# Two graph layers on one core: where the degree search, the edge counts, the sort and three groups of loads stand

## The chip, the cores and the metric

The kernel runs as one program on one core of a Trainium2 chip. The metric is the device time of one execution in microseconds (us); several runs give a median. The profile is of one further execution, taken by the hardware profiler. Its engines are called PE (matmul), PEld (PE's weight loads), DVE (vector), ACT (scalar), POOL (GpSimd) and SP (it only issues transfers); each of them executes its own stream of instructions in order.

## The reference

The input is a graph of 3125 nodes with 256 features and 100,000 directed edges, sorted by their target; the gates have an edge list of their own with 65,536 edges, which isn't sorted. Two layers follow, each of a graph network, a linear attention over all nodes and a group of experts, added to the features:

```python
xn = _layernorm(x, axis=-1)
x = x + _L0_gnn_ref(xn, edge_index, ...) + _L0_mix_ref(xn[None], ...)[0]
x = x + _L0_ffn_ref(_layernorm(x, axis=-1)[None], ..., L0_ffn_edge_index)[0]
xn = _layernorm(x, axis=-1)
x = x + _L1_gnn_ref(xn, edge_index, ...) + _L1_mix_ref(xn[None], ...)[0]
x = x + _L1_ffn_ref(_layernorm(x, axis=-1)[None], ...)[0]
```

A graph network is two convolutions with degrees normalized on both sides (the degree counts a node's incoming edges and itself):

```python
dinv = jnp.where(deg > 0, jax.lax.rsqrt(deg), 0.0)
norm = dinv[src] * dinv[dst]
hw = h @ W
msg = norm[:, None] * hw[src]
return jax.ops.segment_sum(msg, dst, num_segments=n) + b
```

Layer 0's attention is linear: keys and values are summed over all nodes into one context, which every query is multiplied with. Its experts (four, the best two of each node) are chosen by an attention over the gates' edge list. Layer 1's attention takes keys and queries to second order (`einsum('bhni,bhnj,bhne->bhije', kn, kn, vN)`); its eight experts are all computed and weighted by a softmax.

## The kernel before

The nodes are cut into 25 tiles of 128 (NT; the last has 53), and these into seven chunks of four tiles (CHUNKS; the last chunk has one). A convolution is a product with a dense adjacency matrix of edge counts, so it takes 25 steps k of one tile of sources for each chunk of targets. Every engine executes in order; the order is made by a list scheduler from the program, in which generators (`turns(work, n)` runs n steps of a piece of side work) weave side work into the main loops. A pool hands out SBUF from the left or (`**right`) from the right end; a tile that takes the space of an earlier one waits for that one's last readers.

The stages, in order of time in the profiled execution:

- 0 to 20 us: edge keys are made, and where each window of targets begins is searched for (`locate0`; its `find` is a search that counts smaller keys with ACT's Sign, gathers a row for each threshold by an indirect transfer on POOL, and counts in it again; the rows stand in a ring of tiles, `bufs`).
- 20 to 118: the kv phase of layer 0's attention, with LN on ACT (`layernorm(..., True)`), `to_columns`, keys, values and the context; `locate0` goes on beside it, four turns a chunk. Behind it stands `degrees0`: a second `find` with 25 thresholds, from whose counts come the degrees and `dinv`, with three turns of `counts` (the adjacency blocks, stage by stage: masks on DVE, products on PE, casts on ACT, a store to `cols`) for each of its turns.
- 122 to 254: the queries of layer 0's attention, tile by tile, with turns of `counts` and of `merging` (weights multiplied together). `feeder` loads rows of xn in fives and `split`s them, scaled by `dinv`, into a high and a low part (`hs`).
- 260 to 563: conv_1 (`conv_columns`, line 883, then `first_rows`). Ahead of each step k stand a split, the previous chunk's `first_rows`, counts for the next chunk, and the sort of the gates' edges (`sort1`: 512 keys on each of 128 partitions, min and max operations on DVE at lines 609, 610, 619 and 620, and from its tenth round on transposes `s_tp` on PE), `SORT[c]/4` turns a step. When the sort is through, `locate1` stores the keys (`ks1`), searches the windows and gathers them (`b_rows`, `b_got`), and `halves` transposes them (`b_gp`, line 360).
- 604 to about 820: conv_2 (`conv_rows`, line 904), with the counts of the gates' edges as side work. `blocks` and `wide_blocks` load an adjacency block (`adj`, line 856) and cast it (`adj_r`, line 859, ACT).
- 820 to about 1440: gates and four experts.
- 1440 to 1543: `project`: LN, the projections of layer 1's queries, keys and values, norms, and the stores of q, vk and hs to DRAM.
- 1549 to about 1815: mid_1, the first convolution with `key_sums` (products of key pairs, `kk` and `qa`, lines 2004 and 2013) as side work.
- 1815 to 2128: mid_2, the second convolution with layer 1's queries as side work: for each half of a chunk `q0`, four `left` and four `right` blocks are loaded (lines 2050 to 2061) and `gq`, `tt`, `yp` computed.
- 2152 to the end: `experts1`: 24 weight blocks of 0.26 MB on POOL's queue, then the first `prepare` (a load of x, LN, transposes, gates), then the eight experts for each chunk.

`project`, `layer1` and `experts1` are called one after the other; the pools of layer 1 (`l1`, `mid`, `mid_a`, `mid_1`, `mid_2`, `ffn`, `ffn_w`) are on the left, where project's pools are.

Of the kernel before, what the change touches and what calls it, by code (L numbers as in the profile page):

```python
# [17 lines left out]
P = 128  # L18
N = 3125
C = 256  # L20
NT = 25
# [34 lines left out]
PACE = 18  # L56
SORT = (2, 4, 5, 6, 6, 6, 8)
COLS = 782
# [37 lines left out]
def tile_gps_layers(ctx: ExitStack, tc: tile.TileContext, a: dict, out: bass.AP):  # L96
# [365 lines left out]

    def locate0(p, p3, ps, lo, hi, state):


        si = p.tile([P, COLS], I32, name="b_si")
        di = p.tile([P, COLS], I32, name="b_di")
        nxt = p.tile([P, 1], I32, name="b_nxt")
        full = E0 // COLS
        rest = E0 - full * COLS  # L470
        DVE.memset(si, 0)
        DVE.memset(di, N)
        DVE.memset(nxt, N)
        for t, name, queue in ((di, "dst", nc.sync), (si, "src", nc.scalar)):
            for r0, r1 in ((0, 112), (112, full)):
                queue.dma_start(t[r0:r1], a[name][r0 * COLS:r1 * COLS].rearrange("(p c) -> p c", c=COLS))
            queue.dma_start(t[full:full + 1, :rest], a[name][full * COLS:E0].rearrange("(p c) -> p c", p=1))
        with nc.allow_non_contiguous_dma(reason="the first of each row"):
            nc.scalar.dma_start(
                nxt[:full], bass.AP(tensor=a["dst"].tensor, offset=a["dst"].offset + COLS, ap=[[COLS, full], [1, 1]])  # L480
            )
        tabs = tables(p, ps, FAMILIES)
        next(tabs)
        yield

        DVE.tensor_scalar(di, di, N, None, op0=OP.min)
        DVE.tensor_scalar(si, si, N - 1, None, op0=OP.min)
        key = p.tile([P, COLS], F32, name="b_key")
        DVE.scalar_tensor_tensor(key, di, float(NPAD), si, op0=OP.mult, op1=OP.add)
        nc.sync.dma_start(ks[0:P * COLS, :].rearrange("(p c) o -> p (c o)", p=P), key)  # L490
        end = p.tile([P, 32], F32, name="b_end")
        DVE.memset(end, float(N * NPAD))
        nc.sync.dma_start(ks[P * COLS:, :].rearrange("(p c) o -> p (c o)", p=P), end)
        first = firsts(p, ps, key, SEG)
        base, thr, kcol, behind = next(tabs)
        nb = thr.shape[1]
        c = yield from find(p, p3, "w", 10, first, SEG, thr, nb, ks)
        got = gather(p, p3, c, kcol, ks, nb)
        yield
        thr_i = p.tile([P, NT], I32, name="b_thr_i")  # L500
        POOL.iota(thr_i, pattern=[[P, NT]], base=0, channel_multiplier=1)
        thr_n = p.tile([P, NT], F32, name="b_thr_n")
        DVE.tensor_scalar(thr_n, thr_i, float(N), float(NPAD), op0=OP.min, op1=OP.mult)
        yield from halves(p3, ps, got, base, lo, hi, "halves")
        state[:] = first, thr_n, di, nxt, key, got, behind

    def degrees0(p, p3, ps, want, state):

        first, thr_n, di, nxt, key, got, behind = state

# [4 lines left out]
        DVE.tensor_scalar(sh[:, 1], steps, float(P - 1), None, op0=OP.is_equal)  # L517
        c = yield from find(p, p3, "n", 10, first, SEG, thr_n, NT, ks)
        DVE.tensor_copy(begin[:, :NT], c)
# [10 lines left out]
        ranges = summed(FAMILIES)  # L530
        found = p.tile([P, 3 + 2 * len(ranges)], F32, name="b_found")
        wide = p.tile([P, COLS], BF16, name="b_wide")
# [4 lines left out]
        DVE.tensor_tensor(found[:, 1:2], nxt, di[:, COLS - 1:], op=OP.is_lt)  # L537
        over(p, got, behind, found[:, 2:3])
        for i, ends in enumerate(ranges):
# [304 lines left out]
    def wide_blocks(p):  # L844
# [5 lines left out]
        def make(i):  # L850
# [9 lines left out]
            made[i] = r  # L860

        make(0)
        for i, (ts, k0) in enumerate(steps_):
            make(i + 1)
            r = made.pop(i)
            for j in range(5):
                yield k0 + j, r[:, j]

# [605 lines left out]
    def counted(t):  # L1474
        while len(made) <= t and next(counts, 0) is None:
            pass

    with pool("where", **right) as wp, pool("where_w", **right) as wp3, pool("kv") as kp, \
            pool("kv_w", bufs=2) as mw, pool("ps_acc", space=PSUM) as psa:
        found_ = []  # L1480
        work = locate0(wp, wp3, psb, lo_b, hi_b, found_)
        turns(work, 1)
# [6 lines left out]
        for ts in CHUNKS:  # L1489
            xc = load_x(mw, ts)  # L1490
            turns(work, 4)
            xn = layernorm(mw, [xc[:, i, :] for i in range(len(ts))], True)
            ACT.activation(xc[:, :len(ts)], xn[:, :len(ts)], AF.Copy, bias=1.0)
# [21 lines left out]
        for g in range(2):  # L1515
            for h in range(4):
                s = slice(h * HD, (h + 1) * HD)
                DVE.tensor_copy(ctx_sb[s, g, s], ctx_ps[g][s, s])
                DVE.tensor_copy(ctx_sb[s, g, 128 + h:129 + h], ctx_ps[g][s, 128:129])
        for _ in degrees0(wp, wp3, psb, want, found_):  # L1520
            turns(counts, 3)

# [41 lines left out]
    hs = hp_.tile([P, NT, 2, C], F32R, name="hs")  # L1564
    feed = feeder(xp, hs, xn_dram, dinv)
    fed = (feed(k) for k in range(NT))

    with pool("merge") as gm, pool("mix_w", bufs=2) as mw, pool("ps_y", bufs=2, space=PSUM) as psy:
        merging = merged(gm, psm)
        turns(merging, 1)  # L1570
        for ts in CHUNKS:
# [6 lines left out]
            for g in range(2):  # L1578
# [8 lines left out]
                elu1(mw, qT[:, g, :w], qp[:, :w], [P, w])  # L1587
            for i, t in enumerate(ts):
                turns(counts, 1)
                op_ = psm.tile([P, 512], F32, name="op_", tag="a")  # L1590
# [111 lines left out]
    def general():  # L1702

        with pool("gat") as gp:
# [6 lines left out]
            with pool("moe", bufs=5) as mo, pool("moe_w") as ep, pool("moe_b", bufs=2) as mb, \  # L1711
                    pool("ps_e", bufs=2, space=PSUM) as ps:
                for step in moe0(mo, mb, ps, ps, "w", xT, load_e1(ep), *load_e2(ep)):
                    for _ in step:
                        pass
        for _ in project():
            pass
        layer1(False)

# [46 lines left out]
    def project():  # L1766
# [3 lines left out]
        with pool("proj") as pp, pool("proj_w", bufs=2) as cw, pool("ps_pr", bufs=2, space=PSUM) as ps:  # L1770
# [8 lines left out]
            for ts in CHUNKS:  # L1779
                n = len(ts)  # L1780
                c0, w = ts[0] * P, n * P
                xc = bring(cw, x_dram, ts)
                xn = layernorm(cw, [xc[:, i] for i in range(n)])
                xT = cw.tile([P, 2, 512], F32, name="xT")
# [7 lines left out]
                for i, t in enumerate(ts):  # L1792
                    r = rows_of(t)
                    cur = slice(i * P, (i + 1) * P)
                    qp = ps.tile([P, 512], F32, name="qp")
                    hp = ps.tile([P, 512], F32, name="hp")
# [50 lines left out]
    def experts1():  # L1847

        with pool("ffn") as fp, pool("ffn_w", bufs=2) as fw, pool("ps_f", bufs=3, space=PSUM) as ps, \
                pool("ps_fp", bufs=2, space=PSUM) as psp:  # L1850
# [4 lines left out]
            ws = [fp.tile([P, NE1, 2, C], F32, name="w_" + name) for name in names]  # L1855
            for e in range(NE1):
                for name, w in zip(names, ws):
                    nc.gpsimd.dma_start(w[:, e], a[name][e].rearrange("(k p) o -> p k o", p=P))

# [52 lines left out]
            got = []  # L1912
            for _ in prepare(chunks[0], got):
                pass
# [46 lines left out]

    def layer1(fast):
        with pool("l1") as lp:
            wpr = load_w(lp, "m1_wproj", 2)
# [80 lines left out]
            def queries(qw, pst, ps, ts, xc):  # L2045

                n, c0, w = len(ts), ts[0] * P, len(ts) * P
                oT = qw.tile([P, 2, 512], F32, name="oT", bufs=1)
                for g in range(2):
                    qc = q_dram[ts[0] // 4][:, 4 * g:4 * g + 4]  # L2050
                    q0 = qw.tile([P, 512], F32, name="q0", bufs=2)
                    nc.gpsimd.dma_start(q0[:, :w], qc[:HD].rearrange("j h w -> h j w"))

                    def four(name, bufs, at, by):
                        t = qw.tile([P, 4 * 512], F32, name=name, bufs=bufs)[:, :4 * w]
                        nc.gpsimd.dma_start(t, shifted(qc[at:], [HEADS * w, HD], [by * HEADS * w, 4], [1, 4 * w]))
                        return t
# [39 lines left out]

            def layer1_middle(fast):
                with pool("mid") as ch, pool("mid_a", bufs=2) as ca:
                    ahead = None  # L2100
                    if fast:
                        hs = ch.tile([P, NT, 2, C], F32R, name="hs")
                    else:
                        hs = ch.tile([P, NT, C], F32, name="hs_f")
                        hs4 = ch.tile([P, NT, C], F32, name="hs4")

                    def before(k):
                        if first and ahead:
                            ahead(k)
                        turns(work, 1)  # L2110

                    with pool("mid_1", bufs=2) as cw, pool("ps_c1", space=PSUM) as psc, \
                            pool("ps_cw1", bufs=2, space=PSUM) as ps, pool("ps_q1", space=PSUM) as psq:
                        work = key_sums(cw, psq, ps)
                        if fast:
                            ahead = feeder(ca, hs, hs_dram)
                        else:
                            nc.sync.dma_start(hs, hs_dram.rearrange("t p c -> p t c"))
                        gen = wide_blocks(ca) if fast else None
                        for ts in CHUNKS:  # L2120
# [21 lines left out]
                        for _ in work:  # L2142
                            pass
                    with pool("mid_2") as cw, pool("ps_c2", space=PSUM) as psc, \
                            pool("ps_cw2", bufs=2, space=PSUM) as ps, pool("ps_q2", space=PSUM) as pst:
# [19 lines left out]

            layer1_middle(fast)
            experts1()

    for _ in project():
        pass  # L2170
    layer1(True)
    slow = nc.values_load(slow_i[0:1, 0:1], min_val=0, max_val=1)
# [52 lines left out]
```

## Time and profile before

| | us |
|---|---|
| runs | 2729.72, 2735.25, 2735.89 |
| median | 2735.25 |
| the profiled execution's own time | 2732.49 |
| its span in the profile | 2730.7 |
| PE busy | 2492.9 (91%) |
| DVE busy | 1559.6 (57%) |
| ACT busy | 1356.6 (50%) |
| POOL busy | 169.1 (6%) |

The span is the time from the first to the last instruction in the profile; 1.8 us of the execution's time lie around it. The mean granted clock of PE was 0.944 of full speed. The chain that ended last, followed back from the end, is PE for 62% of the span, DVE for 7%, ACT for 5% and transfers for 3%.

Two further stretches are needed for the change, those of conv_1's chunks 0 and 1 (the columns are the stretch, its length, then the busy time and instructions of PE, PEld, DVE, ACT and POOL, the granted clock, the share of the DMA engines and GB/s):

```profile
260.00:280.00 20.00, 18.50 (x123) 14.63 (x123) 16.49 (x38) 9.47 (x9) 2.41 (x5) 0.91 0.55 193
280.00:300.00 20.00, 17.66 (x126) 12.97 (x125) 19.67 (x42) 6.50 (x9) 0.00 (x0) 0.95 0.21 85
300.00:320.00 20.00, 20.00 (x115) 14.19 (x114) 19.12 (x42) 14.10 (x18) 0.00 (x0) 0.97 0.64 205
320.00:340.00 20.00, 20.00 (x177) 15.49 (x176) 19.70 (x36) 13.27 (x24) 0.00 (x0) 1.00 0.37 145
```

The waits are read as a stretch of time in which an engine stood idle ahead of an instruction, with what ended the idling: "PE b_gp L360 <- DMA b_got" is PE, idle before the transposes of line 360, released when the transfer into b_got had landed; behind it are the sum in us, the number of such waits and the longest.

### The profile page before, as it was taken

The numbers are of one execution on the slowest core, as the hardware profiler recorded it, in microseconds if no ns is written. First come the engines' busy times: TensorE is split into PE (matmuls) and PEld (weight loads), VectorE is DVE, ScalarE is ACT, GpSimd is POOL, SyncE is SP. The second block draws the span as 40 slices with busy tenths as digits, with TensorE's granted clock in tenths as the row PEclk, the third lists the DMA queues.
The fourth block names the chain that finished last, engine by engine and source line by source line (L and its number), as shares of the span: only waits on it lengthen the run. The fifth ranks groups of instructions, "written<-read, shape, count | busy, mean of one in ns | idle before, by whom it ended". The sixth has DMA issues, their size and how long they took to land.

```text
span 2730.7 us, 33385 instructions
## 1 busy us (share of the span) xinstructions
PE 2492.9 (91%) x12351; PEld 1556.4 (57%) x12351; DVE 1559.6 (57%) x3626; ACT 1356.6 (50%) x2299; POOL 169.1 (6%) x234
## 2 busy tenths in 40 slices
PE   5788999959888799999979799999999699999999
PEld 3466777747674255555554376664555355555666
DVE  5678966547846756666549845547675422222221
ACT  5734566448857977777733444442332222222332
POOL 4411000010000000000001100011111200000000
PEclk8889999969999899999979899999999799999999
DMA  4434344346553111111015655369784300000000
GB/s 148 142 111 153 141 165 156 102 154 234 207 173 116 46 54 39 54 54 54 23 39 177 228 160 152 121 198 341 265 280 167 130 1 16 14 14 0 14 6 12
DMA packets 192591, 318.44 MB, mean 117 GB/s; under 512 B 12665, under 2 KB 165570, under 8 KB 186274
## 3 DMA queue, kind: packets, MB, share of 16 engines
q1 hardware_dynamic: 170930, 234.58, 26.2%
q0 software_dynamic: 17648, 77.12, 7.9%
q10 hardware_dynamic: 3840, 4.51, 0.5%
q8 instruction: 99, 1.62, 0.2%
q14 instruction: 74, 0.61, 0.1%
HBM read 229.40 MB, written 86.73 MB: 116 GB/s over the span
## 4 chain that ended last, share of the span: by engine, by line
PE 62%; DVE 7%; ACT 5%; DMA 3%; issue 1%; POOL 0%; SPq 0%; ACTq 0%; DVEq 0%; POOLq 0%
PE hp L1927 13%; PE acc L904 9%; PE yp L1139 7%; PE yp L1943 7%; PE acc L883 6%; PE hp L1125 5%; ACT pos L1277 2%; PE qa L2013 2%; PE tt L2084 2%; PE wb_p L1059 1%; PE by_s L1290 1%; PE b_bank L433 1%; DMA adj<-cols 1%; ACT adj_r L859 1%; DVE pos L1281 1%
## 5 line engine op out<-in xcount | busy, mean ns | idle before, releaser
L859 ACT CAST adj_r<-adj 128x2560 fp32r<-128x2560 bf16 (+1 forms) x140 | 293.1, 2104 | 245.8 <-PE acc L883 80.8
L904 PE MATMUL acc<-hs,adj_r 128*128 128x512 f32 (+1 forms) x1250 | 361.0, 420 | 13.3 <-DVE y L922 7.1
L883 PE MATMUL acc<-adj_r,hs 128*128 128x512 f32 (+1 forms) x1400 | 353.8, 398 | 4.2 <-ACT adj_r L859 4.2
L1277 ACT ACTIVATE pos<-drow,a_s 128x512 bf16<-128x512 f32 (+1 forms) x532 | 315.9, 665 | 78.2 <-PE by_s L1290 77.9
L1932 ACT ACTIVATE h<-hp,bn_b,bn_s 128x512 f32<-128x512 f32 (+2 forms) x224 | 160.9, 723 | 367.4 <-PE hp L1927 367.4
L904 PEld LDWEIGHTS acc<-hs,adj_r 128*128 128x128 f32 (+1 forms) x1250 | 224.7, 189 | 117.6 <-issue 54.7
L883 PEld LDWEIGHTS acc<-adj_r,hs 128*128 128x128 f32 x1400 | 248.5, 194 | 62.1 <-issue 8.3
L1946 DVE SCALAR_TENSOR_TENSOR xc<-yp,gate,xc 128x256 f32<-128x256 f32 (+1 forms) x200 | 95.1, 483 | 298.6 <-PE yp L1943 298.5
L1281 DVE TENSOR_TENSOR pos<-pos,adj 128x2048 bf16<-128x2048 bf16 (+1 forms) x133 | 146.9, 1107 | 122.6 <-ACT pos L1277 122.0
L1125 PE MATMUL hp<-g_xT,w 128*128 128x512 f32 (+1 forms) x448 | 195.9, 567 | 15.8 <-ACT hT L1128 14.1
L1139 PE MATMUL yp<-w,hT 128*128 128x256 f32 x800 | 208.4, 413 | 1.0 <-DVE xc_b L1140 1.0
L1943 PE MATMUL yp<-w_f_wo,h 128*128 128x256 f32 (+1 forms) x800 | 194.5, 386 | 0.3 <-ACT h L1932 0.2
L1927 PE MATMUL hp<-h,w_f_w 128*128 128x512 f32 (+2 forms) x448 | 185.8, 545 | 0.3
L1927 PE MATMUL hp<-xT,w_f_w 128*128 128x512 f32 (+2 forms) x448 | 184.0, 548 | 0.0
L403 DVE TENSOR_TENSOR b_ul<-lo_b,upto 128x2048 bf16<-128x2048 bf16 x117 | 143.7, 1228 | 67.8 <-PE b_bank L433 66.6
L1139 PEld LDWEIGHTS yp<-w,hT 128*128 128x128 f32 x800 | 158.8, 205 | 40.7 <-issue 15.9
L455 ACT CAST b_stage<-b_bank 128x500 bf16<-128x500 f32 (+7 forms) x323 | 151.3, 533 | 54.9 <-PE b_bank L433 53.8
L2004 DVE TENSOR_TENSOR kk<-vk 128x512 f32<-128x512 f32 (+1 forms) x200 | 125.6, 685 | 91.3 <-issue 51.3
L1943 PEld LDWEIGHTS yp<-w_f_wo,h 128*128 128x128 f32 (+1 forms) x800 | 142.5, 187 | 48.4 <-ACT h L1932 13.2
L433 PE MATMUL b_bank<-b_uh,b_ul 128*128 128x125 bf16 (+5 forms) x1856 | 139.6, 215 | 29.3 <-DVE b_uh L408 21.8
L433 PEld LDWEIGHTS <-b_ul 128*128 128x128 bf16 x1856 | 105.0, 102 | 81.7 <-issue 52.9
L1927 PEld LDWEIGHTS hp<-h,w_f_w 128*128 128x128 f32 x448 | 81.9, 190 | 94.0 <-issue 39.5
(566 smaller groups left out, 3446.9 us busy)
## 6 DMA issues: line engine op xcount, KB each, us to landing
adj<-cols SPq DMA_DIRECT2D x150, 640.0 KB, 4.6
cols<-b_stage SPq DMA_DIRECT2D x50, 800.0 KB, 4.5
left<-q_dram POOLq DMA_DIRECT2D x24, 1024.0 KB
right<-q_dram POOLq DMA_DIRECT2D x24, 1024.0 KB
xs_n<-hs_dram SPq DMA_DIRECT2D x15, 640.0 KB, 5.7
vk<-vk_dram SPq DMA_DIRECT2D x10, 840.0 KB, 4.8
vk_dram<-vk SPq DMA_DIRECT2D x6, 1344.0 KB, 5.0
x_in<-in_x SPq DMA_DIRECT2D x12, 512.0 KB, 6.1
```

Of the source, the lines that this page charges most:

```text
L433: PE.matmul(bank[:, n * NT:(n + w) * NT], u[:, i // 2, :, i % 2], v[:, i // 2, :NT * w, i % 2], start=k == 0, stop=k == room - 1,)
L455: ACT.copy(dst, src)
L859: ACT.copy(dst, src)
L883: PE.matmul(acc[f][:, :w], hs[:, k, q, s], at[:, :len(ts)], start=k == 0 and q == 0, stop=k == NT - 1 and q == 1,)
L904: PE.matmul(acc[i][:r, :], at[:, i, :r], hs[:, k].rearrange("p q c -> p (q c)"), start=k == 0, stop=k == NT - 1,)
L1125: PE.matmul(hp[:, :w], w1[:, e, k, f * P:(f + 1) * P], xT[:, k, c0:c0 + w], start=k == 0, stop=k == 1)
L1139: PE.matmul(yp[:, :C], hT[:, f, i * P:(i + 1) * P], w2[:, e, f, :], start=f == 0, stop=f == 3)
L1277: ACT.activation(pos[:, h, :n].rearrange("p t d -> p (t d)"), drow[:, h, :w], AF.Sign, bias=a_s[:, k, h:h + 1],)
L1281: DVE.tensor_mul(pos[:, :, :n], pos[:, :, :n], at[:, None].to_broadcast([P, 4, n, P]))
L1927: PE.matmul(hp[:, :w], ws[layer][:, e, k, f * P:(f + 1) * P], h[:, k, :w], start=k == 0, stop=k == 1,)
L1932: ACT.activation(hn[:, f, :w], hp[:, :w], AF.Relu, bias=bn[layer][1][:, at:at + 1], scale=bn[layer][0][:, at:at + 1],)
L1943: PE.matmul(yp[:r, :C], h[:, k, i * P:i * P + r], ws[2][:, e, k, :], start=k == 0, stop=k == 1)
```

## The change

Five things are moved; what is computed stays the same.

1. The sort of the gates' edges gets more turns in each of conv_1's chunks (SORT), so it stands earlier in the order.
2. `degrees0` is a generator that is now run one turn for each tile of the queries, and its tiles and those it takes over from `locate0` come from a pool of their own (`degrees`, `pd`); its ring of rows has 6 tiles and not 10. `over` (a check of the windows) moves into `locate0`. The counts that stood with the degrees are run in the kv phase instead, four turns a chunk from tile 12 on, and LN of the first three chunks there is done on DVE. The feeder is made when its first turn is asked for.
3. Layer 1's pools go to the right end. `project` is a generator that is run for six of its seven chunks; then layer 1's pools are opened, the feeder and the first adjacency block are made, and only then the seventh chunk is run. `project`'s LN goes to ACT, and the first tile's `qp` is taken ahead of LN.
4. The ten loads of the first chunk's queries in mid_2 go from POOL's queue to SP's.
5. The 24 weight loads of `experts1` go from POOL's queue to SP's, and stand behind the first step of the first `prepare` (the load of x and LN) in the program.

```diff
-SORT = (2, 4, 5, 6, 6, 6, 8)
+SORT = (4, 5, 7, 7, 8, 8, 8)
...
-    def locate0(p, p3, ps, lo, hi, state):
+    def locate0(p, p3, pd, ps, lo, hi, state):
...
+        found = pd.tile([P, 3 + 2 * len(summed(FAMILIES))], F32, name="b_found")
+        over(p, got, behind, found[:, 2:3])
+        state[:] = first, thr_n, di, nxt, key, found
...
-        c = yield from find(p, p3, "n", 10, first, SEG, thr_n, NT, ks)
+        c = yield from find(p, p3, "n", 6, first, SEG, thr_n, NT, ks)
...
+        def each():
+            for i, (ts, k0) in enumerate(steps_):
+                make(i + 1)
+                r = made.pop(i)
+                for j in range(5):
+                    yield k0 + j, r[:, j]
+
         make(0)
-        for i, (ts, k0) in enumerate(steps_):
-            make(i + 1)
-            r = made.pop(i)
-            for j in range(5):
-                yield k0 + j, r[:, j]
+        return each()
...
             turns(work, 4)
-            xn = layernorm(mw, [xc[:, i, :] for i in range(len(ts))], True)
+            if ts[0] >= 12:
+                turns(counts, 4)
+            xn = layernorm(mw, [xc[:, i, :] for i in range(len(ts))], ts[0] >= 12)
...
-        for _ in degrees0(wp, wp3, psb, want, found_):
-            turns(counts, 3)
+        for _ in work:
+            pass
...
-    feed = feeder(xp, hs, xn_dram, dinv)
-    fed = (feed(k) for k in range(NT))
+
+    def feeding():
+        feed = feeder(xp, hs, xn_dram, dinv)
+        for k in range(NT):
+            feed(k)
+            yield
+
+    fed = feeding()
...
+        degrees = degrees0(wd, wd, psb, want, found_)
...
             for i, t in enumerate(ts):
+                turns(degrees, 1)
                 turns(counts, 1)
...
-                xn = layernorm(cw, [xc[:, i] for i in range(n)])
+                qp = ps.tile([P, 512], F32, name="qp")
+                xn = layernorm(cw, [xc[:, i] for i in range(n)], True)
...
-            for e in range(NE1):
-                for name, w in zip(names, ws):
-                    nc.gpsimd.dma_start(w[:, e], a[name][e].rearrange("(k p) o -> p k o", p=P))
...
-            for _ in prepare(chunks[0], got):
+            first = prepare(chunks[0], got)
+            next(first)
+            for e in range(NE1):
+                for name, w in zip(names, ws):
+                    nc.sync.dma_start(w[:, e], a[name][e].rearrange("(k p) o -> p k o", p=P))
+            for _ in first:
                 pass
...
+                    queue = nc.gpsimd if ts[0] else nc.sync
...
-                        nc.gpsimd.dma_start(t, shifted(qc[at:], [HEADS * w, HD], [by * HEADS * w, 4], [1, 4 * w]))
+                        queue.dma_start(t, shifted(qc[at:], [HEADS * w, HD], [by * HEADS * w, 4], [1, 4 * w]))
...
+                    if fast:
+                        ahead = feeder(ca, hs, hs_dram)
+                        gen = wide_blocks(ca)
+                    for _ in rest:
+                        pass
...
-    for _ in project():
-        pass
-    layer1(True)
+    maps = project()
+    turns(maps, len(CHUNKS) - 1)
+    layer1(True, maps)
```

## The prediction

> **What bounds the kernel now.** I read the busy shares first, then the stretches where they drop, then the waits and the chain in those. PE works 91% of the span:
>
> ```profile
> span 2730.7 us, 33385 instructions
> PE 2492.9 (91%) x12351; PEld 1556.4 (57%) x12351; DVE 1559.6 (57%) x3626; ACT 1356.6 (50%) x2299; POOL 169.1 (6%) x234
> PE   5788999959888799999979799999999699999999
> PEclk8889999969999899999979899999999799999999
> ```
>
> Outside the first 120 us, PE's digits dip at slices 8, 20 to 22 and 31: the turn from conv_1 to conv_2 in layer 0 (from 560 us), from project to the first convolution of layer 1 (from 1540) and from mid_2 to the experts (from 2128). There is also a shallower stretch after the kv phase (120 to 160). The stretches themselves (columns: span; busy time of PE, PEld, DVE, ACT, POOL; granted clock; DMA share; GB/s):
>
> ```profile
> 120.00:140.00 20.00, 10.26 (x85) 6.45 (x84) 14.38 (x36) 8.88 (x24) 13.30 (x8) 0.68 0.65 221
> ...
> 560.00:580.00 20.00, 7.36 (x32) 6.18 (x31) 7.23 (x28) 6.59 (x23) 4.83 (x5) 0.67 0.41 140
> 580.00:600.00 20.00, 4.71 (x25) 3.02 (x26) 10.96 (x28) 5.42 (x15) 4.82 (x6) 0.50 0.40 122
> 600.00:620.00 20.00, 17.93 (x103) 13.72 (x101) 8.93 (x10) 14.89 (x19) 0.00 (x0) 0.79 0.54 182
> ...
> 1540.00:1550.00 10.00, 4.46 (x34) 2.64 (x38) 7.11 (x23) 3.04 (x7) 0.63 (x1) 0.68 0.59 222
> 1550.00:1560.00 10.00, 6.41 (x148) 3.43 (x144) 8.90 (x20) 2.88 (x9) 0.00 (x0) 0.98 0.79 263
> 1560.00:1570.00 10.00, 6.01 (x32) 3.10 (x25) 10.00 (x24) 7.99 (x14) 0.00 (x0) 0.54 1.00 339
> ...
> 2140.00:2150.00 10.00, 0.00 (x0) 0.00 (x0) 2.34 (x15) 0.00 (x0) 7.74 (x11) 0.50 1.04 348
> ```
>
> No engine is full where PE idles, so these are waits. What ended them, PE's waits at 520 to 606 and at 2120 to 2166, with two steps of the chain:
>
> ```profile
> PE b_gp L360 <- DMA b_got<-ks,b_ci: 20.8, 5, 17.6
> PE s_tp L648 <- DVE s_key L610: 5.5, 2, 4.0
> ...
> PE tr L187 <- DVE ln_xn L176: 23.6, 1, 23.6
> ...
> 1825.72 16.22 DMA q<-q_dram
> ...
> 2131.36 18.30 DMA xc<-x_dram
> ```
>
> After the sort's last stage (565.0 us) come the store of the keys, two rounds of gathers and the table products; only then does conv_2's first matmul (604.43) get its block. At the end of mid_2, LN waits for an 18.3 us load of x's rows.
>
> **The change, part by part.**
>
> *Sort sooner.* SORT[c]/4 turns per k step, 25 steps a chunk: 12, 25, 31, 37, 37, 37, 50 before, 229 in all; now 25, 31, 43, 43, 50, 50, 50, or 292. The sort has 229 yields and the search 16 more; the sum passes 229 thirteen turns before chunk 5 ends and 245 just after. In the built program the gathers stand 4 to 8 matmuls into chunk 6 (of 50). Before, chunk 5 ended about 528 and the sort 565, and its tail took 565 to 592.7, the b_gp wait's end: 27.7 us. Started at 528 it ends near 556, before chunk 6 (563). What still stands before conv_2 is the last hw2 (569.55), adj's load (4.6 us by the DMA issues) and a cast of 2.23: 576.4 instead of 604.4. PE's idle in 560 to 620 is 12.64 + 15.29 + 2.07 = 30.0; about 7 stay, so I take 24. Upper bound 35 (all idle, and the 5.5 of s_tp waits). Lower bound 8: in SP's order adj now stands behind two xc loads, a store of hs, xs_n and a store of cols1, and three landings of 5 us in a row would add 15.
> The price: a stage is two DVE operations, 0.417 to 0.421 us each (L609, L610), so 0.84. Chunk 0 gets 13 more turns: 10.9 us, where DVE was idle only 3.5 + 0.3 of 260 to 300. That is 7 us late, between 0 (PE has 1.5 and 2.3 idle there already) and 10.9. Chunks 2 to 5 gain 6 to 13 turns each, under 11 us, against DVE's 24 to 30 busy of 40: hidden. If not, PE stops at the transposes s_tp, which stand in its own order. Net 17.
>
> *Degrees amid queries, counts amid keys.* The degree search moves 25 gathers (POOL), 100 small ACT operations (0.51, 0.20, 0.63, 0.19: 38 us) and its three DVE steps from the end of the kv phase into the queries; 16 turns of counts move into the kv phase, and LN of the first three chunks from ACT to DVE. PE's idle in 120 to 160 is 9.74 + 4.67 = 14.4, the most there is. But DVE is busy 17 to 19 of each 20 us from 160 to 260, so degrees must stay cheap there, and the built program still issues all 25 gathers before the kv phase ends, with dinv ready ten feed steps later than before. I take 6, between 15 and -5: POOL and ACT stand at 0 and 9.5 of 20 after 140 and dinv is needed only from 250 on, but the 5.6 us that DVE idles in 120 to 140 are then lost to a search that lands on a full DVE. The ring of gather tiles falls from 10 to 6, cost nothing under the same idle POOL.
>
> *Layer 1's pools and project's last tile.* Six chunks of project, then the feeder's loads, splits and the first adj load and cast, then the one-tile chunk. In the built order PE goes from project's last transposes straight to acc. Idle in 1540 to 1570 is 5.54 + 3.59 + 3.99 = 13.1. Ten hs splits (0.42 us each, 4.2 in all) move into a project whose DVE has 9.8 of each 10 us busy: I take 12 less 2. LN moves there from DVE to ACT (25 x 0.43, L176 there, = 10.7 us off DVE; on ACT 25 x 0.56, L174 in the kv phase, = 14.0, hidden under its 4.3 of 10): PE idles only some 5%, so 2. Net 12, between 5 and 17.
>
> *First queries on SP.* Ten loads, 2 x (0.25 + 4 x 1.02) = 8.7 MB, leave POOL's queue for SP's, behind hs's store and xc, ahead of xs_n and the fifth adj. POOL was held until 1824.11; on SP they can go from about 1819. But 8.7 MB at the 348 GB/s shown above is 25 us either way, and SP stops at the fourth `right` until DVE frees a buffer, so xs_n and adj come some 10 us later. I take 2, between -5 and 6. The Trainium skill (DMA: Bandwidth & Descriptors, "Issuing engines are not separate DMA queues") says that SP, ACT and GpSimd feed the same 16 DMA engines, so that another issuer saves issue time alone; the stretch at a share of 1.04 agrees, and by that rule this part would be worth 0.
>
> *Experts' start.* 24 weight loads of 0.26 MB leave POOL for SP. Before they shared the DMA engines with three xc loads, all issued from 2130.18; LN's last input landed at 2149.8. Now eight of them stand ahead of the first xc on SP, the other xc's behind all 24. Eight are 2.1 MB or 6.0 us at 348 GB/s; they can begin at 2127.2 (the last acc), xc adds 0.5 MB or 1.5, so it lands near 2135 and at worst, behind a wait of SP for the last row's store (3.5 us there), near 2139: 15 or 11 us sooner. Allow 3 to 15 and take 10: the clock stays cold at such a gap (0.50 there). The Trainium skill (TensorE: Matmul & The Clock Gate, "What's actually happening") puts the drop to half rate at about 3.4 us of idling. By that rule too the 10 us that remain bring no gain of clock here, while the gap at 1560, closed whole, would.
> Clock: the 6 us of work at 0.54 in 1560 to 1570 at full speed save 2.8. I add 3.
>
> Sum: 17 + 6 + 12 + 2 + 10 + 3 = 50. The profiled execution was 2732.49 (1.8 around its span), 2.8 under the median 2735.25; 2732.5 - 50 = 2682.5, on the median's footing 2685.
>
> **The rivals.**
> 1. *The sort's tail only shrinks*: adj behind SP's row of loads (the lower bound 8) and DVE's lateness of 10.9 eat that part, and the experts' xc gains only 3: 50 - 20 - 7 = 23, so 2712. For it: SP's in-order queue. Against: the loads ahead are not blocked in 555 to 570.
> 2. *Everything arrives*: the upper bounds, 35 - 7 + 15 + 17 + 6 + 15 + 3 = 84, so 2651. For it: PE is the only full engine, and all of this is its idle time. Against: DVE's 97% in 280 to 340, and the 10 us that the experts' first load takes in any case.
> 3. *The degrees do not move in effect*, since their gathers still stand in the kv phase: that term 0, 2691.
> 4. *Slower*: the denser sort makes PE wait at its transposes. Fourteen s_tp groups (seven rounds of two) stand in PE's order; one wait was 4.0 us at worst, with 50 turns a chunk. If all fourteen pay that, 56, and chunk 0 pays 10.9 instead of 7, the sum is 50 - 56 - 4 = -10: 2745. It decides from 3.6 us per transpose on. For it: chunks 4 to 6 now all run at 50 turns. Against: only 2 of 14 waited in 520 to 606, when nothing was left behind them, and DVE has 10 to 15 us of 40 free in chunks 2 to 5.
>
> **Numbers.** My forecast 0.55 (2670 to 2702, with rival 3 inside it), rival 1 0.22, rival 2 0.10, rival 4 0.08, and 0.05 for the terms adding up to nothing. The range 2655 to 2715 takes in rival 1 and reaches almost to rival 2; it leaves out rival 4, the nothing case and the edges of the others. A measurement here tells apart about 0.3%, 8 us. Faster 0.88, same 0.04, slower 0.08.
>
> **What would show it.** conv_2's first acc 24 to 30 us after conv_1's last, not 41, with b_gp's wait under 3 us; s_tp waits under 10 us in all (above 40, rival 4); acc of mid_1 right after project's last transposes; PE's wait for ln_xn before the experts 10 to 15 us; and the kv phase's end followed by a stretch with less than 7 of 20 us idle on PE. I am wrong if the queries grow by more than 6 us or if mid_2's start waits longer for xs_n than it gains.

## The result, and the profile after

The changed kernel took 2700.65 us (median of four runs, 2691.64 to 2711.03); the kernel before, run beside it, 2732.48. The ratio is 0.9886, with a 95% interval from 0.9843 to 0.9929. The profiled execution took 2696.51 us, 36.0 less than that of before (2732.49). One thing ahead of the rest: the text on the kernel before says four `left` and four `right` loads for each half of a chunk; it is two and two, each of four shifted blocks (1.02 MB).

The page of the changed kernel, its busy times and slices:

```profile
span 2694.7 us, 33358 instructions
PE 2488.3 (92%) x12351; PEld 1548.0 (57%) x12351; DVE 1558.3 (58%) x3617; ACT 1362.4 (51%) x2312; POOL 143.6 (5%) x200
...
PE   5887999889988899999879999989999799999998
```

PE has nearly the work that it had (2488.3 us against 2492.9); its idle time fell from 237.8 us to 206.4. Counted from 0, slice 8 has gone from 5 to 8, and the 7s of slices 20 and 22 have shrunk to one; slice 26, in mid_2, has a new 8 among 9s. The stages' ends, from the two traces' PE records (us of the span):

| | before | changed | moved |
|---|---|---|---|
| kv phase, last ctx ends | 118.5 | 120.0 | +1.5 |
| queries, last ty ends | 254.6 | 235.2 | -19.4 |
| conv_1, first acc starts | 260.2 | 249.4 | -10.8 |
| conv_1, last acc ends | 561.0 | 552.7 | -8.3 |
| conv_2, first acc starts | 604.4 | 573.2 | -31.2 |
| conv_2, last acc ends | 838.2 | 804.4 | -33.8 |
| gates, last by_s ends | 1415.5 | 1380.6 | -34.9 |
| mid_1, second chunk ends | 1632.9 | 1597.1 | -35.8 |
| mid_1, last acc ends | 1815.2 | 1775.5 | -39.7 |
| mid_2, last acc ends | 2126.9 | 2101.1 | -25.8 |
| experts, first gate product | 2154.1 | 2118.9 | -35.2 |
| end of the last yp | 2724.2 | 2687.9 | -36.3 |

Read by differences: 10.8 us came from the front; conv_1 grew by 2.5; 25.5 came between conv_1's end and conv_2's, 22.9 of them at the turn; 1.1 came in the gates, next to nothing (0.9) from project and mid_1's start, 3.9 in the rest of mid_1; mid_2 lost 13.9; and the experts' start brought 9.4 to their first product, 10.5 to the end.

Stretches of the changed kernel that answer to those shown of before (same columns), and PE's waits in 500 to 575, in 1770 to 1852 and in 2095 to 2125:

```profile
120.00:130.00 10.00, 7.78 (x29) 3.87 (x29) 8.38 (x24) 2.81 (x6) 3.65 (x2) 0.66 0.71 255
130.00:140.00 10.00, 9.20 (x87) 7.20 (x84) 9.13 (x29) 3.02 (x7) 1.47 (x1) 1.00 0.01 2
...
540.00:560.00 20.00, 17.52 (x129) 16.44 (x129) 11.78 (x28) 10.51 (x28) 0.96 (x1) 0.93 0.76 250
560.00:580.00 20.00, 14.65 (x91) 10.99 (x90) 9.44 (x10) 13.45 (x21) 0.00 (x0) 0.81 0.73 240
...
1510.00:1520.00 10.00, 4.75 (x18) 2.33 (x16) 8.84 (x30) 3.88 (x11) 0.63 (x1) 0.82 0.52 185
1520.00:1530.00 10.00, 10.00 (x46) 8.17 (x46) 1.45 (x5) 3.65 (x5) 0.00 (x0) 0.84 0.58 209
...
1820.00:1830.00 10.00, 5.65 (x28) 0.88 (x27) 10.00 (x5) 0.78 (x3) 1.80 (x3) 0.83 0.98 306
```

```profile
PE b_gp L360 <- DMA b_got<-ks,b_ci: 3.7, 3, 2.4
...
PE gq L2080 <- DMA q<-q_dram: 6.2, 2, 5.3
PE tt L2101 <- DVE qq L2092: 3.5, 4, 1.4
...
PE tr L187 <- DVE ln_xn L176: 14.1, 1, 14.1
```

The wait for the gathers fell from 20.8 us to 3.7 and the wait before the experts from 23.6 to 14.1. PE is busy at 1520, where before it idled until 1566. But at 1820 it is half idle at a DMA share of 0.98. The chain of waits in mid_2's first chunk shows why:

```profile
1783.90 18.70 DMA q<-q_dram
1802.60 28.29 DMA adj<-cols
1830.89 0.02 issue
1830.91 2.33 ACT adj_r L859
```

An adj load that takes 4.2 us at the median took 28.3 here: it was issued on SP behind the ten loads of queries, and beside the next chunk's on POOL.

### The profile page after: what moved, and what is told of

The parts are those of the page before. It is cut to its first block, busy times and chain, and to the rows that moved or that the text cites. A ratio compares the mean times of both kernels' runs of the same rounds, so it can differ in the third digit from the quotient of the medians.

```text
span 2694.7 us, 33358 instructions
## 1 busy us (share of the span) xinstructions
PE 2488.3 (92%) x12351; PEld 1548.0 (57%) x12351; DVE 1558.3 (58%) x3617; ACT 1362.4 (51%) x2312; POOL 143.6 (5%) x200
## 4 chain that ended last, share of the span: by engine, by line
PE 62%; DVE 7%; ACT 5%; DMA 4%; issue 1%; SPq 0%; ACTq 0%; DVEq 0%
PE hp L1943 13%; PE acc L907 9%; PE yp L1142 7%; PE yp L1959 7%; PE acc L886 6%; PE hp L1128 5%; DMA adj<-cols 3%; PE qa L2029 2%; ACT pos L1280 2%; PE tt L2101 1%; PE wb_p L1062 1%; PE by_s L1293 1%; ACT adj_r L859 1%; PE b_bank L433 1%; DVE pos L1284 1%
## 5 line engine op out<-in xcount | busy, mean ns | idle before, releaser
L886 PEld LDWEIGHTS acc<-adj_r,hs 128*128 128x128 f32 x1400 | 245.4, 192 | 63.7 <-issue 13.1
L1128 PE MATMUL hp<-g_xT,w 128*128 128x512 f32 (+1 forms) x448 | 195.4, 566 | 15.1 <-ACT hT L1131 13.4
```

The lines of the kernel that those rows point to most:

```text
L886: PE.matmul(acc[f][:, :w], hs[:, k, q, s], at[:, :len(ts)], start=k == 0 and q == 0, stop=k == NT - 1 and q == 1,)
L1128: PE.matmul(hp[:, :w], w1[:, e, k, f * P:(f + 1) * P], xT[:, k, c0:c0 + w], start=k == 0, stop=k == 1)
```

## The experiments

Stage lengths are those of each run's profile. "Gates to mid_1" is the stretch from the gates' end to the end of mid_1's second chunk (before 217.5, changed 216.5), "first two" the length of mid_2's first two chunks (109.2 and 124.0). Where a time is set beside the changed kernel's, "the eight runs" are those four and four of e4, which has the same order of instructions (median 2707.9).

**e1.** The queries' loads back on POOL:

```diff
-                    queue = nc.gpsimd if ts[0] else nc.sync
+                    queue = nc.gpsimd
```

> The changed kernel with the ten loads of mid_2's first query chunk back on POOL's queue; all else as changed. In the changed kernel mid_2's chunk 0 took 71.8 us (1777.0 to 1848.8) against 41.6 before, and one adj load there took 28.3 us; over mid_2 11 us were lost. Theory A: on SP the ten loads (8.7 MB) stand ahead of xs_n and adj, so the convolution waits for them; back on POOL's queue chunk 0 takes 40 to 48 us, no adj load there over 12 us on the chain, and the time falls by 8 to 12 us. Theory B: the loss comes from mid_1's earlier end (all stores and loads of the turn falling together at the DMA engines' limit); then chunk 0 still takes over 60 us and the time changes by less than 4 us.

Measured: 2712.97 us (ratio to before 0.9918, interval 0.9889 to 0.9946). mid_2's first chunk 59.9 us, the first two 129.1, mid_2 342.7. Theory A failed: with the pools where the change puts them, POOL's queue is no better. Theory B came in part: the first chunk is just under its 60 us, but the time is 12.3 us above the changed kernel's (5.1 above the eight runs), where under 4 was said. SP's waits in 1770 to 1815, then POOL's, then those of the kernel before (SP's and POOL's in 1810 to 1850):

```profile
SPq L703 <- DMA hs_dram<-new: 21.2, 1, 21.2
...
POOL left L2073 <- DVE h4T L2149: 259.5, 1, 259.5
```

```profile
SPq L703 <- DMA hs_dram<-new: 4.5, 1, 4.5
...
POOL left L2056 <- DMA hs_dram<-new: 25.2, 1, 25.2
```

Before, POOL's second `left` waited for mid_1's last store of hs, because of the space that it took; so the store (0.13 MB) went without the queries, in 4.5 us, and xs_n followed; only q0 and the first `left` had gone out earlier. With the pools at the right end the same load waits for another reader (`h4T`), is free 3.6 us ahead of the store, and the store, which SP waits for before xs_n, takes 21.2 us beside 6.4 MB of queries (seven loads; the expectation of e5 counts 4.3 MB).

**e2.** The sort's old turns:

```diff
-SORT = (4, 5, 7, 7, 8, 8, 8)
+SORT = (2, 4, 5, 6, 6, 6, 8)
```

> The changed kernel with the old turns for the sort (2, 4, 5, 6, 6, 6, 8). Theory A: the sort's tail comes back behind conv_1: conv_2's first acc 40 to 44 us after conv_1's last (20.5 in the changed kernel), and conv_1 becomes 1 to 3 us shorter: the time rises by 20 to 25 us. Theory B: a good part of the 25 us comes from degrees and counts being out of the way sooner; then the gap is under 35 us and the time rises by less than 15 us.

Measured: 2727.38 us (0.9984, 0.9964 to 1.0003). From conv_1's last acc to conv_2's first 41.1 us (20.5 changed, 43.4 before), conv_2's end 19.4 us later, conv_1 299.7 us long against 303.3. PE's wait for b_got in 500 to 592 is back:

```profile
PE b_gp L360 <- DMA b_got<-ks,b_ci: 18.7, 4, 16.4
PE s_tp L648 <- DVE s_key L610: 5.8, 2, 4.4
```

Theory A: the tail is the sort's alone; the time rises by 26.7 us, by 19.5 against the eight runs. The denser sort's price in conv_1 is 3.6 us, and it falls into chunk 1 (54.6 us in the changed kernel, 48.0 here), not into chunk 0 (30.8 and 32.2).

**e3.** Degrees, counts, the kv phase's LN and the feeder as before (all hunks of part 2 undone).

> The changed kernel with degrees0, counts, the kv phase's LN and the feeder as before. In the changed kernel the last ty of the queries ends 19.4 us sooner, conv_1's first acc 10.8 us sooner and its last 8.3 us sooner. Theory A: this part is worth what conv_1's first acc shows: first acc near 260 us, the time 8 to 11 us longer. Theory B: conv_1's start is set by DVE's queue of counts, not by the queries; what comes sooner there is paid back by conv_1's end, and the time rises by less than 5 us.

Measured: 2723.29 us (0.9956, 0.9933 to 0.9979). conv_1's first acc at 257.9 (+8.5), its last at 566.0 (+13.3), conv_2's end 9.1 us later: theory A, for the stages. The profiled execution is 26.1 us longer than the changed kernel's, and the rest stands in stages of which this edit changes no line: 9.9 in mid_2 (335.5 us against 325.6), 4.1 in the gates, 2.9 in the experts.

**e4.** Project run whole:

```diff
-    turns(maps, len(CHUNKS) - 1)
+    turns(maps, len(CHUNKS))
```

> The changed kernel with all seven chunks of project run before layer 1's pools are opened (the pools stay at the right end, LN stays on ACT). In the changed kernel the stretch from the gates' end to the end of mid_1's chunk 1 takes 216.5 us against 217.4 before: the idle time of PE between project and mid_1 is gone, but project is 6.4 us longer. Theory A: the two belong together: with the feeder's splits and loads behind project again, project is 4 to 7 us shorter and the gap comes back, the time changes by less than 3 us. Theory B: the longer project is due to LN on ACT alone, and the weaving is worth the whole gap: the time rises by 7 to 12 us.

Measured: 2712.09 us (0.9911, 0.988 to 0.9941), gates to mid_1 216.1. The scheduler made the same streams from it (the same on DVE and SP; on PE and ACT only a weight tile's number differs), so neither theory was tried: writing the last chunk behind the feeder changes no order. The run is worth more as a repetition. Its mid_2 took 340.2 us, the changed kernel's 325.6, from the same order of instructions. The eight runs of the two have a median of 2707.9, so by the medians the change is worth rather 24 to 32 us than 36.

**e5.** The queries on POOL, with a dependency of the first half's five loads on that store:

```diff
+                    if not (ts[0] or g):
+                        after(load, kept)
...
+                                kept[:] = [nc.sync.dma_start(
+                                    hs_dram[ts[0]:ts[0] + n].rearrange("t p c -> p t c"), new[:, :n]
+                                )]
```

> The changed kernel with the first queries' ten loads on POOL's queue, the five of the first half made to wait for mid_1's last store of hs. With them on POOL's queue and no such wait, mid_2 took 342.7 us (from mid_1's last acc to mid_2's last), 325.6 in the changed kernel, 311.7 before; there the store of hs took 21.2 us behind 4.3 MB of query loads that had started 3.6 us ahead of it (4.5 before, where POOL itself had waited 25.2 us for that store), and xs_n waited for the store. Theory A: what counts is that the store and xs_n are not behind the queries' data; the store takes under 7 us, mid_2 takes 308 to 318 us and the time falls by 8 to 14 us against the changed kernel. Theory B: mid_2 is longer for a reason that this order does not touch (where its tiles now lie, the loads' rate); it takes 325 us or more again.

Measured: 2705.87 us (0.9905, 0.9869 to 0.994). The store's wait was 4.5 us again and the first chunk 51.7 us (73.3 changed), but the second took 72.4: first two 124.1, mid_2 333.4, in the range of theory B (325 or more). Theory A fails as it was put. Part of that lies in the edit: q0 waited for the store too; ACT then stood 8.5 us before an operation on q0 and with it the casts of adj.

**e6.** Layer 1's pools at the left end again, opened when project's are closed (`turns(maps, len(CHUNKS) + 1)` and `**right` taken from l1, mid, mid_a, mid_1 and mid_2), queries on POOL.

> The changed kernel with layer 1's pools (l1, mid, mid_a, mid_1, mid_2) at the left end again and opened behind all of project, and the first queries on POOL's queue; LN of project stays on ACT, the experts' pools at the right end. Theory A: the place of the pools is what did both: closed the gap between project and mid_1 and let the queries' loads start ahead of the store of hs. So the gap is back (first acc 149 to 153 us after the gates' end, 139.6 in the changed kernel), project itself is shorter by 4 to 7 us, the gates' end to mid_1's second chunk takes 215 to 219 us as in both kernels, and mid_2 takes 308 to 318 us: the time falls by 8 to 14 us against the changed kernel. Theory B: the pools' place closed the gap for nothing else: the stretch to mid_1's second chunk is 223 us or more, and mid_2's gain is eaten.

Measured: 2690.04 us (2686.02 to 2696.8; 0.9836, 0.9818 to 0.9854). The first acc is 154.9 us after the gates' end, gates to mid_1 221.2, the first two 115.6, mid_2 317.4. Both halves of theory A came, the gap and mid_2's gain, but three of its figures were missed: the first acc is later than 149 to 153, project is only 2.5 us shorter (last qp at 126.7 against 129.2, 4 to 7 said), and gates to mid_1 is over 219. So 4.7 us are lost to mid_1, but mid_2 gains more. The waits are those of before: POOL's in 1782 to 1830, PE's in 1500 to 1545, and PE's of the kernel before in 1536 to 1570:

```profile
POOL left L2073 <- DMA hs_dram<-new: 25.6, 1, 25.6
...
PE qa L2029 <- DVE kk L2020: 6.4, 6, 2.1
PE tr L187 <- DVE qf L1845: 5.2, 4, 4.2
...
PE qa L2013 <- DVE kk L2004: 7.6, 7, 2.1
PE tr L187 <- DVE qf L1831: 5.5, 5, 4.2
```

**e7.** The experts' weights on POOL's queue, ahead of `prepare`, as before.

> The changed kernel with the experts' 24 weight loads on POOL's queue and at their old place in the program. In the changed kernel the stretch from mid_2's last acc to the experts' first gate product is 17.8 us, 27.3 before. Theory A: the queue decides, since on SP the first load of x has only eight weights ahead of it, and on POOL all 24 share the DMA engines with it: 26 to 29 us, the time 8 to 11 us longer. Theory B: it is the experts' pools at the right end that let loads start sooner: 17 to 21 us, and the time within 3 us of the changed kernel's.

Measured: 2719.64 us (0.9938, 0.9914 to 0.9962). From mid_2's last acc to the first gate product 27.8 us (17.8 changed): theory A for this stretch. Of the 27.0 us by which the profiled execution is longer, the other 16.5 stand in mid_2 (342.1), which comes ahead of these loads. PE's wait in 2112 to 2150, and the step of the chain:

```profile
PE tr L187 <- DVE ln_xn L176: 24.1, 1, 24.1
...
2122.26 18.95 DMA xc<-x_dram
```

In the changed kernel the same load of x took 5.81 us of the chain.

**e8.** No counts in the kv phase:

```diff
-            if ts[0] >= 12:
-                turns(counts, 4)
```

> The changed kernel without the four turns of counts a chunk in the kv phase, so that these 16 turns fall to the queries and conv_1; degrees as changed. In the changed kernel the kv phase ends 1.5 us later, the queries 19.4 us sooner and conv_1's first acc 10.8 us sooner than before. Theory A: the queries are bound by DVE and the counts moved under the kv phase are what shortened them: the queries end 10 us or more later than in the changed kernel, conv_1's first acc 5 to 12 us later. Theory B: the degrees' waits, gone from the turn between the phases, are what shortened them: the queries end less than 5 us later and conv_1 starts less than 4 us later.

Measured: 2726.88 us (0.9985, 0.9959 to 1.001). The kv phase ends 8.3 us sooner (111.7), the queries at 235.9, hardly later, but conv_1's first acc comes at 268.9, 19.5 us later. So B for the queries and more than A for conv_1. Three stretches in between and PE's wait in 230 to 272:

```profile
240.00:250.00 10.00, 4.22 (x51) 3.84 (x49) 10.00 (x23) 0.00 (x0) 0.00 (x0) 0.50 0.16 51
250.00:260.00 10.00, 4.75 (x80) 4.41 (x79) 9.94 (x28) 3.32 (x7) 0.00 (x0) 0.50 0.33 135
260.00:270.00 10.00, 3.59 (x51) 3.29 (x52) 10.00 (x19) 5.12 (x5) 0.00 (x0) 0.50 0.50 164
```

```profile
PE b_bank L433 <- DVE b_uh L408: 19.5, 13, 3.2
```

DVE is full (10 of 10 us), most of it with the masks of the counts that conv_1 must have. What decides conv_1's start is this queue, not the queries. The rest of part 2 by itself would have made it later than before (268.9 against 260.2); the counts under the kv phase, for 8.3 us there, save 19.5.

**e9.** The kernel of e6 with project's LN on DVE (the `True` of the diff taken out).

> The kernel of e6 (layer 1's pools at the left end behind project, first queries on POOL's queue) with project's LN on DVE as before. In e6 project's last qp starts 126.7 us after the gates' end, in the kernel before 122.8, with no hs splits woven in in either. Theory A: LN on ACT costs project some 4 us, because the first LN then stands behind two weight loads that ACT issues (one waited for) and ACT's casts; with LN on DVE 122 to 124 us, and the gates' end to mid_1's second chunk 216 to 218.5 (221.2 in e6): 3 to 5 us less time. Theory B: the 4 us come from elsewhere, and LN on DVE, with DVE at 98% there, is no shorter: 126 us or more.

Measured: 2689.5 us (2681.83 to 2694.43; 0.9827, 0.9802 to 0.9853). Last qp at 125.1, gates to mid_1 219.0: 2.2 us less than e6, under the 3 to 5 that A had said (its other two ranges are missed by 1.1 and 0.5), and no difference in the time that could be measured. mid_2 took 311.7, as before.

**e10.** mid_2's pool alone at the left end, the rest of layer 1's at the right, queries on POOL.

> The changed kernel with the first queries on POOL's queue and mid_2's own pool alone at the left end, where project's tiles lay, the rest of layer 1 at the right end. The tiles of the queries then take space that is free from project's end on, not mid_1's. Theory A: the first queries' 8.7 MB load during mid_1, where the DMA engines' share is below 0.6, and the turn to mid_2 no longer has to share them: mid_2's first two chunks take 95 to 105 us (109.3 before, 124.0 in the changed kernel, 115.6 in e6) and mid_2 296 to 310; the time falls by 15 to 25 us against the changed kernel. Theory B: the loads are held by something else (the queue's order, the pool's opening), or the loss lies in the later loads: first two chunks 115 us or more, time within 8 us of e6's.

Measured: 2707.33 us (0.991, 0.9877 to 0.9943). q0 and the first `left` went out at 1516.9 and 1517.6, during mid_1; the second `left` waited 262.0 us for `h4T` all the same, until 1780. First two 130.9: theory A failed, and it is theory B's 115 or more, though the time is 17.3 us above e6's, not within 8. The loads are held by a reader of mid_1's `h4T`; that this is for space that both share follows from the pools' rule and was not looked at. SP waits 21.2 us for the store again.

**e11.** e10 with project's LN on DVE.

> The kernel of e10 with project's LN on DVE. Theory A (LN on ACT costs about 4 us by its wait): 3 to 5 us less than e10, the gates' end to mid_1's second chunk 212 to 214 us (216.5 in the changed kernel). Theory B: here the hs splits are woven into project and DVE is full, so LN on DVE (10.7 us) shows: 218 us or more, and the time is longer than e10's.

Measured: 2708.49 us (0.9896, 0.9868 to 0.9923). Gates to mid_1 214.3 against 218.4 in e10 and 216.5 in the changed kernel; the last qp is at 126.1 against 129.3: theory A for project (214.3 where at most 214 was said), though mid_2 (332.2) hides it in the time, which is not below e10's. ACT's wait ahead of the first LN in 1395 to 1404, in the changed kernel and in e6, and PE's waits behind it, in e10 (1381 to 1600) and e11 (1386 to 1601):

```profile
ACT ln_xn L174 <- DMA w_g_w<-in_g_w: 12.1, 1, 12.1
...
ACT ln_xn L174 <- DVE ln_off L171: 10.6, 1, 10.6
...
PE tr L187 <- ACT ln_xn L174: 4.2, 1, 4.2
...
PE tr L187 <- DVE ln_xn L176: 3.8, 1, 3.8
```

The profile puts the first of these to a weight of layer 1, which ACT itself had issued just ahead. That is not the price of LN on ACT: `ln_off`, an input of that LN, ended on DVE at 1401.58, 0.04 us before LN began. In e6 no such weight stands there and LN on ACT still costs 2.2 us (e9); and PE's wait ahead of the first transposes is only 0.4 us shorter in e11 than in e10. The rest of the 4.1 us comes later in project, and no run shows from what.

**e12.** As e5, but only the loads from the second `left` on wait for the store, and LN on DVE.

> The changed kernel with the first queries on POOL's queue, only the second left load and the loads after it made to wait for mid_1's last store of hs (q0 and the first left go out early, as they do in e6 and in the kernel before), and project's LN on DVE. In e5, where q0 waited too, ACT stood 8.5 us before an operation on q0 and held the casts behind it; mid_2's first chunk took 51.7 us, the first two 124.1 (109.3 before, 124.0 in the changed kernel, 115.6 in e6, 109.9 in e9). Theory A: small and early loads first, the rest behind the store, is all that the left end's waits did: first two chunks 106 to 118 us; with the gates' end to mid_1's second chunk at 213 to 216 us the time is 2680 to 2690 us, at or below e9's 2689.5. Theory B: the right end itself costs mid_2: first two chunks 122 us or more, and the time is 2695 us or more.

Measured: 2707.95 us (0.9889, 0.9867 to 0.9911). Gates to mid_1 214.8, the first two 110.2: both as theory A said, but the time is not (2680 to 2690 was said, and B's 2695 or more came). In the profiled execution, 2713.43, the fourth chunk took 61.8 us instead of 47.4, and the kv phase ended 13.4 us later than in the changed kernel; without the two it would be near 2686, an estimate. The other four runs (2697.26 to 2708.29) have no profile, so what held them is not shown. PE's wait and SP's in the fourth chunk:

```profile
PE acc L907 <- ACT adj_r L859: 9.9, 1, 9.9
...
SPq L856 <- DMA adj<-cols: 21.9, 2, 20.4
```

## Why the prediction was right, and where it was not

Direction and size: 2685 was forecast and 2700.65 measured, inside 2655 to 2715; of the 50 us of the sum, 36 arrived in the profiled execution and 32 in the medians. The terms, though, missed in both directions, and that the sum fell inside the range is in part luck: up to conv_2's end 33.8 us came where 23 were said, and that made up for part of what layer 1's pools and queries fell short by. One of the named signs of being wrong came in substance: mid_2's start lost more than it gained, in waits for q and adj more than for xs_n. The time is not far from rival 1's 2712, but neither of its conditions came.

- *Sort sooner*, net 17: right in mechanism, mis-sized in price. The turn to conv_2 took 20.5 us, 22.9 less than before (24 said; the 41 of the text took conv_1's end at 563, where the trace has 561.0), and b_gp's wait was 3.7 us (under 3 said). The 13 extra stages in chunk 0 were priced at 7; conv_1 grew by 2.5 us, by 3.6 against e2, and that in chunk 1, whose six extra stages had no price. Rival 4 didn't come: PE's waits of 250 to 553 hold no s_tp at all.
- *Degrees and counts*, 6: 10.8 at conv_1's start, 9.1 at conv_2's end (e3); inside the bounds, but well above the term. The reason that I gave (idle time of PE in 120 to 160) is half of it. It is gone, and the queries end 19.4 us sooner, but 8.6 us of that are given back between the queries and conv_1, where DVE works off counts. e8 shows the counts to be the larger lever.
- *Layer 1's pools and project's last tile*, 12, and 3 for the clock: this step failed; about 1 arrived by mid_1's second chunk, 4.8 by mid_1's end. "Idle in 1540 to 1570 is 5.54 + 3.59 + 3.99 = 13.1" was counted as gained, on the reading that no engine is full where PE idles. But the row of 1560 to 1570 has DVE at 10.00 of 10 us, and 7.6 of the idle time were waits for `kk`, the key pairs that DVE makes for `key_sums`: work, not an empty wait. PE did stop idling there, with the first acc 11.6 us sooner after the gates. Before, though, that stretch was where `key_sums` made its first products (184 of its matmuls stand ahead of the first acc, 8 in the changed kernel), while mid_1's first chunk took 27.6 us; now those fall into it and it takes 37.6. And project itself grew by 6.4 us: twenty of the feeder's splits stand in it, not ten, and LN on ACT costs 2 to 4 us (e9 and e11). What was left of the gain came at the other end: mid_1's last chunk takes 20.8 us, and 24.1 to 24.5 in the three profiles with the pools at the left (before, e6, e9). And what set the order at this turn was the pools' place alone: e4 runs project whole and has the same order.
- *First queries on SP*, 2, bounds -5 to 6: this step failed too. mid_2 lost 13.9. I had the delay ("xs_n and adj come some 10 us later") and counted nothing for it. Back on POOL's queue it is no better (e1), because of what I missed one part earlier: the pools' move to the right end took away a wait of POOL, and that wait had kept 7.4 of the queries' 8.7 MB behind a small store and xs_n. With the pools at the left end the first two chunks take 115.6 and 109.8 (e6, e9), and with the order forced at the right end 110.2 (e12); in the nine profiles with mid's pools at the right and no such order they take 123.7 to 132.4. SP's queue with the pools at the left was not run, so what the queue costs by itself stays open.
- *Experts' start*, 10: right; 10.5 in the end, 10.0 in e7, and the wait before them 14.1 us (10 to 15 said).

So the kernel of e9, which keeps the sort, the degrees and counts and the experts' loads, and leaves layer 1's pools (but for the experts'), the queries' queue and project's LN as they were, takes 2689.5 us. That is 11 us under the changed kernel's median; its five runs (to 2694.43) lie below all but one of the eight of the changed kernel's order.

What stays open: why the later chunks of mid_2 are disturbed when mid's pools lie at the right end. In the three profiles with the pools at the left (before, e6, e9) chunks 3 to 7 of mid_2 take 201.8 to 202.4 us together; in the eleven with mid's pools at the right 201.7 to 217.8, in e4 207.8 with the very order that took 201.7 in the changed kernel. Three profiles are few to say so. In e12 and in e9 the adj load in question is issued at nearly the same time beside the same loads; no run tried what makes the one late.

## What to carry to other kernels

Idle time of an engine between two stages is worth what its next work would not have to do later: look at which side work fills the gap now, and where that goes when the gap closes. A wait that a buffer's space imposes can be an order of transfers that the kernel lives by; before moving a pool, list what each load of the next stage waited for, and set the order that counts by a dependency of its own. And where an engine runs full between two phases (DVE with the counts here), the place to take its work is the phase before, where it cost 8.3 us here and saved 19.5, not the one that waits for it.

## What the runs showed of the hardware

A store of 0.13 MB on SP's queue took SP's wait from 4.5 to 21.2 us when 6.4 MB of loads went out on POOL's queue, the first of them 3.6 us ahead of it (e1, e10). The trace's packets show how. From 1778 to 1797 in e1 (queue 0 is POOL's, queue 1 SP's; packets, MB, share of the 16 engines):

```profile
q0 software_dynamic: 992, 5.44, 80.0%
q1 hardware_dynamic: 983, 1.23, 22.2%
```

The two queues moved nearly the same number of packets, but most of POOL's (632) are of 8192 bytes and most of SP's (948) of 1280, so SP's queue got less than a fifth of the bytes. In it two adj loads of 0.64 MB stood ahead of the store (issued at 1775.05 and 1777.28). The store's own packets, of 1024 bytes, begin 19.1 us after its issue; before, 3.1. So it is the store's turn that is late, and a small transfer is not kept safe from a large one on another queue. The Trainium skill (DMA: Bandwidth & Descriptors, "Queues, rings and completion order") says that each DMA engine takes turns, packet by packet, between the queues that have work. The counts of packets agree (992 and 983). At the experts' start of before it is the same: from 2126 to 2150, 1633 packets and 5.39 MB of the weights' queue stand beside 1728 and 1.70 MB of SP's, where x was loaded.

The same order of instructions took 325.6 and 340.2 us for mid_2 in two executions (the changed kernel and e4), 124.0 and 132.4 for its first two chunks. That scatter is more than the effect of most of the edits here, and stage lengths from several profiles told them apart where the medians couldn't.
